# A token-shift layer: who turns the tokens, and on which engine the gate mixture is summed

## The chip, the cores and the metric

The kernel runs on one core of a Trainium2 chip. The metric is the device time of one launch in microseconds. Shown are the median of three runs and, for the profile, one execution taken by the hardware profiler.

The engines are named as the profile names them: PE (TensorE, matrix products), PEld (its weight loads), DVE (VectorE), ACT (ScalarE), POOL (GpSimd) and SP (SyncE, which issues the DMAs). Each works through a queue of its own in order, and waits where an operation needs something that another engine has not delivered yet.

## The reference, cut to what matters

Four layers stand one behind the other, each added to x (8 batches of 512 tokens, 512 features): a cross-attention, a routed feed-forward layer, a masked cross-attention, and the token-shift layer, which the change is about. All is float32.

```python
x_prev = jnp.concatenate([jnp.zeros((B, 1, C)), x[:, :-1, :]], axis=1)
xr = mu_r * x + (1.0 - mu_r) * x_prev          # gate mixture
xk = mu_k * x + (1.0 - mu_k) * x_prev          # key mixture
r = sigmoid(einsum('btc,dc->btd', xr, W_r))    # gates
k_act = square(relu(einsum('btc,dc->btd', xk, W_k)))   # keys
out = r * einsum('btc,dc->btd', k_act, W_v)    # values
...
x = x + tanh(g_ffn[1]) * _L1_ffn_ref(_layernorm(x), W_r, W_k, W_v, mu_r, mu_k)
```

## The kernel before, in words

x stays in SBUF for the whole launch: 32 tiles of 128 tokens by 512 features, four tiles (TB) to a batch. The class ChannelMix is the token-shift layer. It begins inside the second attention: its method in_slot is called from the attention's slots (one slot for each tile; the last four slots and a few behind them are the attention's tail, lines 977 to 994) and prepares batch 0 there. Then mix.run (line 1650) takes the eight batches alone, one after another.

For a batch the layer needs the normalized tokens with features on the partitions. Method normalize (1492) lets ACT write (x - mean) / deviation into a tile xn (line 1500). Method transpose (1504) turns a tile with four PE transposes into one PSUM bank (1514), and ACT copies the bank into yT (1515), a tile of 4 chunks of 128 features by 513 columns whose column 0 is zero, set by POOL (1510): column t+1 holds token t, so that the columns from 0 are the previous tokens and the columns from 1 the tokens themselves. A mixture is made chunk by chunk (mix_chunk, 1517): ACT scales the previous tokens by 1 - mu (1528, "om" is 1 - mu), DVE adds mu times the tokens (1531). xr is the gate mixture, xk the key mixture.

Each of the three 512x512x512 products of a batch (keys, gates, values, in this order) is made by seven products of half the size instead of eight (class SevenProducts). They need sums of quarters of one operand, made beforehand: xks of the key mixture and xrs of the gate mixture (lines 91 to 97 and 107 to 117 make them, so the profile gives them as L91 and L110), wvs of the squared keys. The seven are called p1, p2, p6, p5, p7, p4, p3 in the order in which they run. Each fills one PSUM bank with four matmuls (line 165; the profile counts eight, two passes each) and is taken out of it: p1 and p5 by an ACT copy (177, 192), p2, p6, p7, p4 and p3 by a DVE addition (183, 188, 198, 212, 217). Behind p7, POOL makes two more additions (203, 204); L212 needs the first of them and L217 the second. p6 needs the second sum of its operand's quarters, p5 the first, p7 the third, and p3 or p4 the fourth. Six banks go round.

When a quarter of a product is complete, a function finishes it: the keys get Relu and Square on ACT (1582, 1583), the gates Sigmoid on ACT (1593), the values are multiplied by the gate and r on DVE (1606), added to x on POOL (1609) and, for two quarters together, stored by SP (1618).

The order of the work is written out by hand. A list of seven "turns" holds the steps that are issued behind each of the seven products; method turns (1634) deals a list of steps out evenly, stage (1643) issues them. In run, for batch b:

- key product of b: the four chunks of xr of b (ACT and DVE), then the four sums xrs on DVE; in batches 1 to 4 also the mean and variance (lines 52, 53) of one tile of a later batch behind p2;
- gate product of b: the four sums wvs on DVE, the transposes of the four tiles of b + 1 behind p2, p6, p5 and p7, and the chunks of xk of b + 1;
- value product of b: the four sums xks of b + 1 on DVE, and the normalization of the four tiles of b + 2 on ACT; in batches 0 to 3 the mean and variance of one more tile.

The engines' queues follow this order; SP's queue alone is ordered by the framework. Batch 1 is an exception: its four tiles are normalized behind the attention, at the end of its tail, after the weight sums of the gates (line 1460). The two tiles that hold the normalized tokens of a batch (xn2, two token tiles each) take the places of the attention's v0 and v1.

```python
if b > 0:
    turns = self.turns(chunks(b, 0) + sums(b, 0))
...
for n, step in enumerate(calls(self.transpose, *tiles)):
    turns[n + 1].append(step)
...
work += sums(b + 1, 1)
work += calls(self.normalize, *[(TB * (b + 2) + i,) for i in range(TB)])
```

Of the kernel before, what the change touches and what calls it, by code (L numbers as in the profile page):

```python
# [9 lines left out]
FP = mybir.dt.float32  # L10
I32 = mybir.dt.int32
BF = mybir.dt.bfloat16
AF = mybir.ActivationFunctionType
# [4 lines left out]
P = 128  # L18
B, S, D = 8, 512, 512
LK = 120  # L20
NH, HD = 16, 32
NT = B * S // P
TB = S // P
NC = D // P
# [196 lines left out]
class CrossAttention:  # L221
# [676 lines left out]
    def run(self):  # L898
        for k in range(TB, NT - TB):
            self.steady(k)  # L900
# [96 lines left out]
class RoutedFfn:  # L997
# [101 lines left out]
    def in_slot(self, s, attention, stage):  # L1099

        if stage == "final":
            self.put_aside(s)
            self.route_stats(s)
        if stage == "late":
            self.route_scale(s)
        if stage == 2 and 0 <= s - 1:
            self.route_stats(s - 1)
            self.route_norm(s - 1)
        if stage not in (1, "route"):
            return  # L1110
        pool = attention.p_mm
        if s == -1:
            self.start()
        if stage == "route":
            s -= 1
        if 0 <= s - 4:
            self.route_logits(s - 4, pool.tile([P, D], FP, name="rlps", tag="mm"))
        if 0 <= s - 3:
            self.route_x(s - 3, pool.tile([P, D], FP, name="rxps", tag="mm"))
        b, i = divmod(s - 8, TB)  # L1120
        if i == 0 and 0 <= b < B - 2:
            self.route_back(b, pool.tile([P, D], FP, name="pps", tag="mm"))
# [256 lines left out]
class ChannelMix:  # L1379
# [16 lines left out]
    def start(self):  # L1396
        nc = self.nc
        wr_in, wk_in, wv_in, mu_in = self.ins
        self.pool = pool = self.es.enter_context(
            self.tc.tile_pool(name="cm_w", bufs=1, side="right", reuse_waits="tile")  # L1400
        )
        self.mu = pool.tile([P, 2, NC], FP, name="mu")
        nc.sync.dma_start(out=self.mu, in_=mu_in)
        self.om = pool.tile([P, 2, NC], FP, name="om")
        self.wk = self.load(pool.tile([P, NC, D], FP, name="wk"), wk_in)
        self.wr = self.load(pool.tile([P, NC, D], FP, name="wr"), wr_in)

    def load(self, w, w_in):
        self.nc.sync.dma_start(out=w, in_=w_in.rearrange("(c p) f -> p c f", p=P))
# [26 lines left out]
    def in_slot(self, s, attention, stage):  # L1436

        nc = self.nc
        self.at = attention
        if stage == 2 and s >= 1:  # L1440
            attention.stats(s - 1)
        if stage == "final" and s < NT - 2 * TB:
            attention.stats(s, False)
        if stage == "late" and s < NT - 2 * TB:
            attention.scales(s)
        if s == -1:
            self.start()
        if stage == "head" and s == NT:
            self.sum_value_weights()
            self.k7.next()  # L1450
        if stage == "end" and s == NT + 1:
            for c in range(NC):
                self.mix_chunk(0, 0, c)
            self.k7.next()
        if stage == "end" and s == NT + 2:
            for step in self.sum_steps(0, 0):
                step()
            self.k7.next(2)
            self.sum_gate_weights()
            for t in range(TB, 2 * TB):  # L1460
                self.normalize(t)
        if stage != "route":
            return
        if s == TB + 1:
            nc.vector.tensor_scalar(self.om, self.mu, -1.0, 1.0, ALU.mult, ALU.add)
        i = s - (NT - 9)
        if 0 <= i - 1 < TB:
            self.transpose(i - 1)
        if 0 <= i < TB:
            xn = self.at.norm.tile([P, D], FP, name="xn")  # L1470
            self.normalize(i, xn)
        if s == NT - 4:
            wv = self.at.pool.tile([P, NC, D], FP, name="wv", tag="wq")
            self.wv = self.load(wv, self.ins[2])
            self.weight_sums = self.sum_key_weights()
        if 0 <= s - (NT - 5) < NC:
            self.mix_chunk(0, 1, s - (NT - 5))
        if s in (NT - 4, NT - 3):
            for _ in range(2):
                self.weight_sums.pop(0)()  # L1480
        if s == NT - 2:
            self.key_sums = self.sum_steps(0, 1, nc.gpsimd)
        if s in (NT - 2, NT - 1):
            for _ in range(2):
                self.key_sums.pop(0)()
        if s == NT - 1:
            self.k7 = self.keys(0)
            self.k7.next()
        if s in (NT, NT + 1):
            self.k7.next()  # L1490

    def normalize(self, t, xn=None):
        nc, cm = self.nc, self.cm
        if xn is None:
            i = t % TB
            if i % 2 == 0:
                self.two = self.at.pool.tile([P, 2, D], FP, name="xn2", tag=f"v{i // 2}")
            xn = self.two[:, i % 2, :]
        self.xn[t] = xn
        nc.scalar.activation(  # L1500
            xn, cm.x[:, t, :], AF.Identity, bias=cm.nmr[:, t, :], scale=cm.rstd[:, t, :]
        )

    def transpose(self, t):

        nc = self.nc
        b, i = divmod(t, TB)
        if i == 0:
            self.yT[b] = self.at.work.tile([P, NC, S + 1], FP, name="yT", tag="xnT")
            nc.gpsimd.memset(self.yT[b][:, :, 0:1], 0.0)  # L1510
        xn = self.xn.pop(t)
        ps = self.bank((NC, P))
        for c in range(NC):
            nc.tensor.transpose(ps[:, c, :], xn[:, c * P : (c + 1) * P], self.cm.ident)
        nc.scalar.copy(self.yT[b][:, :, i * P + 1 : (i + 1) * P + 1], ps)

    def mix_chunk(self, b, m, c):

        nc, yT = self.nc, self.yT[b]
        if c == 0:  # L1520
            if m == 1:
                xm = self.at.work.tile([P, NC, S], FP, name="xk", tag="qT")
            else:
                xm = self.at.soft.tile([P, NC * S], FP, name="xr", tag="pr")
                xm = xm.rearrange("p (c s) -> p c s", c=NC)
            self.mix[b, m] = xm
        xm = self.mix[b, m]
        nc.scalar.activation(  # L1528
            xm[:, c, :], yT[:, c, 0:S], AF.Copy, scale=self.om[:, m, c : c + 1]
        )  # L1530
        nc.vector.scalar_tensor_tensor(  # L1531
            xm[:, c, :],
            yT[:, c, 1 : S + 1],
            self.mu[:, m, c : c + 1],
            xm[:, c, :],
            ALU.mult,
            ALU.add,
        )
# [111 lines left out]
    def run(self):  # L1650
        def calls(f, *args):
            return [lambda a=a: f(*a) for a in args]

        def chunks(b, m):
            return calls(self.mix_chunk, *[(b, m, c) for c in range(NC)])

        def sums(b, m):

            steps = []

            def step():
                if not steps:
                    steps.extend(self.sum_steps(b, m))
                steps.pop(0)()

            return [step] * 4

        self.alone = True

        late = NT - 2 * TB  # L1670
        for b in range(B):
            if b > 0:
                turns = self.turns(chunks(b, 0) + sums(b, 0))
                if b <= TB:
                    turns[1].insert(0, lambda t=late + 2 * b - 1: self.at.stats(t))
                self.stage(self.keys(b), turns)
            more = b + 1 < B
            squares = SevenProducts.left_steps(self.kT, *self.kTs, self.nc.vector)
            squares = self.in_order_of_use(squares)
            turns = [[] for _ in range(7)]  # L1680
            for n, step in enumerate(squares):
                turns[n + 2].append(step)
            if more:
                tiles = [(TB * (b + 1) + i,) for i in range(TB)]
                for n, step in enumerate(calls(self.transpose, *tiles)):
                    turns[n + 1].append(step)
                for n, step in enumerate(chunks(b + 1, 1)):
                    turns[5 + n // 2].append(step)
            self.stage(self.gates(b), turns)
            work = []  # L1690
            if more:
                work += sums(b + 1, 1)
            if b + 2 < B:
                work += calls(self.normalize, *[(TB * (b + 2) + i,) for i in range(TB)])
            work = self.turns(work)
            if b < TB:
                work[4].insert(0, lambda t=late + 2 * b: self.at.stats(t))
            self.stage(self.values(b), work)
# [128 lines left out]
```

## Time and profile before

| what | value |
|---|---|
| median of 3 runs | 1346.69 us (1346.25 to 1348.43) |
| the profiled execution, device time | 1344.31 us |
| its span | 1342.5 us |
| PE busy | 1291.0 us, 96% of the span |
| DVE, ACT, POOL busy | 1002.2, 807.1, 704.6 us |
| second attention's tail and what lies around it | about 977 to 1043 us |
| batches 0 to 7 of the token-shift layer alone | about 1039 to 1342 us |

Busy time of an engine is the sum over its instructions; at PE they overlap, and their ends are modelled. In the rows of a timeline or a chain the first number is the start in microseconds from the span's start, the second the length. Where a row ends in square brackets, these hold the idle time of the engine just before the instruction and what ended it. The chain follows the work back from its end: at each step to the instruction that released the waiting one or to the one before it on its engine. "issue" is time in which a queue waits for nothing that the profile shows.

### The profile page before, as it was taken

The numbers are of one execution on the slowest core, as the hardware profiler recorded it, in microseconds if no ns is written. First come the engines' busy times: TensorE is split into PE (matmuls) and PEld (weight loads), VectorE is DVE, ScalarE is ACT, GpSimd is POOL, SyncE is SP. The second block draws the span as 40 slices with busy tenths as digits, with TensorE's granted clock in tenths as the row PEclk, the third lists the DMA queues.
The fourth block names the chain that finished last, engine by engine and source line by source line (L and its number), as shares of the span: only waits on it lengthen the run. The fifth ranks groups of instructions, "written<-read, shape, count | busy, mean of one in ns | idle before, by whom it ended". The sixth has DMA issues, their size and how long they took to land. (4 is left out here: it accounts for less than half of the span.)

```text
span 1342.5 us, 32823 instructions
## 1 busy us (share of the span) xinstructions
PE 1291.0 (96%) x13184; PEld 1024.3 (76%) x13184; DVE 1002.2 (75%) x1448; ACT 807.1 (60%) x2540; POOL 704.6 (52%) x626
## 2 busy tenths in 40 slices
PE   7999999999999988999999999999999999999997
PEld 6886777777766877888888667667666888888886
DVE  5876776777685776777887687777785778787776
ACT  1368888888774445455136778888774655544442
POOL 4856655565542002555797787777664333343332
PEclk9999999999999999999999999999999999999999
DMA  9501766766603256431410077767700000000000
GB/s 313 189 1 66 224 208 204 222 211 208 198 26 111 86 171 199 128 112 63 154 47 18 33 229 214 220 212 222 223 23 1 16 17 32 32 32 32 32 32 32
DMA packets 116237, 160.84 MB, mean 120 GB/s; under 512 B 6973, under 2 KB 71997, under 8 KB 116085
## 3 DMA queue, kind: packets, MB, share of 16 engines
q1 hardware_dynamic: 116085, 158.75, 37.1%
q8 instruction: 104, 1.70, 0.5%
q14 instruction: 48, 0.39, 0.1%
HBM read 93.84 MB, written 64.88 MB: 118 GB/s over the span
## 5 line engine op out<-in xcount | busy, mean ns | idle before, releaser
L721 ACT ACTIVATE pr<-s,nmx 128x120 f32<-128x120 f32 x768 | 273.5, 498 | 43.4 <-DVE nmx L710 25.1
L878 PE MATMUL ops<-wo,aT 128*128 128x512 f32 x512 | 237.0, 604 | 3.6 <-ACT aT L869 2.3
L731 POOL TENSOR_TENSOR pr<-pr,rs 128x960 f32<-128x960 f32 x88 | 160.1, 1820 | 139.9 <-DVE rs L727 138.0
L721 ACT ACTIVATION_READ_ACCUMULATOR pr<-s,nmx 128x1 f32 x768 | 195.3, 254 | 0.0
L878 PEld LDWEIGHTS ops<-wo,aT 128*128 128x128 f32 x512 | 91.9, 189 | 99.8 <-issue 89.2
L710 DVE TENSOR_REDUCE nmx<-s 128x8 f32<-128x960 f32 x96 | 106.6, 1153 | 57.9 <-PE s L666 57.8
L1353 POOL TENSOR_TENSOR r<-r,b 128x1024 f32<-128x1024 f32 x31 | 73.5, 2377 | 145.1 <-ACT r L1352 145.1
L793 DVE STREAM_TRANSPOSE pr<-pr 128x1024 f32<-128x1024 f32 x88 | 109.1, 1240 | 37.0 <-POOL pr L731 37.0
L165 PE MATMUL qps<-xnT,wq 128*128 128x256 f32 x512 | 119.0, 380 | 0.0
L165 PEld LDWEIGHTS qps<-xnT,wq 128*128 128x128 f32 x512 | 96.3, 189 | 23.3 <-issue 10.3
L52 DVE BATCH_NORM_STATS2 bnst<-x 128x6 f32<-128x512 f32 x128 | 87.5, 684 | 0.4
L1609 POOL TENSOR_TENSOR x<-x,cv 128x512 f32<-128x512 f32 x30 | 44.0, 1466 | 79.0 <-DVE cv L1606 79.0
L759 POOL TENSOR_TENSOR pr<-pr,rs 128x960 f32<-128x960 f32 x32 | 58.1, 1823 | 40.6 <-DVE rs L758 30.8
L861 PE MATMUL aps<-prT,v 120*32 120x128 f32 x2048 | 69.2, 276 | 7.6 <-DMA prT<-plane 3.9
L888 DVE SCALAR_TENSOR_TENSOR x<-ops,gates,x 128x512 f32<-128x512 f32 x64 | 47.8, 746 | 34.5 <-PE ops L878 34.1
L666 PE MATMUL s<-kT,qT 32*128 32x120 f32 x2048 | 71.8, 276 | 0.0
L666 PEld LDWEIGHTS s<-kT,qT 32*128 32x128 f32 x2048 | 65.7, 186 | 7.0 <-issue 4.9
L861 PEld LDWEIGHTS aps<-prT,v 120*32 120x32 f32 x2048 | 52.2, 109 | 21.2 <-issue 10.7
L1352 ACT COPY r<-rps 128x1024 f32<-128x1024 f32 x31 | 31.4, 1013 | 59.1 <-PE rps L1340 59.1
L1582 ACT ACTIVATE kT<-kT 128x512 f32<-128x512 f32 x32 | 20.0, 626 | 76.2 <-DVE kT L183 41.8
L1340 PE MATMUL rps<-ident,rT 128*128 128x128 f32 x512 | 61.9, 275 | 2.0 <-DVE rT L1320 1.7
L769 ACT ACTIVATE pr<-s,nmx 128x120 f32<-128x120 f32 x128 | 44.2, 371 | 29.0 <-DVE nmx L766 29.0
(239 smaller groups left out, 3134.4 us busy)
## 6 DMA issues: line engine op xcount, KB each, us to landing
plane<-pr SPq DMA_DIRECT2D x88, 512.0 KB, 3.5
prT<-plane SPq DMA_DIRECT2D x176, 240.0 KB, 4.1
w<-in_w_dram SPq DMA_DIRECT2D x32, 512.0 KB, 5.0
x<-in_x_dram SPq DMA_DIRECT2D x8, 1024.0 KB, 16.6
aside<-x SPq DMA_DIRECT2D x32, 256.0 KB, 3.1
x<-aside SPq DMA_DIRECT2D x8, 1024.0 KB, 9.7
out_dram<-x SPq DMA_DIRECT2D x14, 512.0 KB, 2.8
wk<-in_wk_dram SPq DMA_DIRECT2D x3, 1024.0 KB, 8.8
```

The costliest lines, as they stand in the source:

```text
L52: cm.nc.vector.bn_stats(st, cm.x[:, t, :])
L165: self.nc.tensor.matmul(ps[:, m, :], rows[:, k, m * n : (m + 1) * n], columns[:, k, :], start=(k == 0), stop=(k == 1),)
L666: nc.tensor.matmul(s[j // 2][:, j % 2, hc * LK : (hc + 1) * LK], self.qT[b][r : r + 32, hc, toks], self.kT[r : r + 32, hc, keys], start=no ...
L710: nc.vector.tensor_reduce(nmx[u], sv[u], AX.X, ALU.max, negate=True)
L721: nc.scalar.activation(dst, src, AF.Exp, bias=nmx[u][:, j, hc, :], accum_out=sm[:, u, j, hc : hc + 1],)
L731: nc.gpsimd.tensor_tensor(half[u], half[u], by, ALU.mult)
L759: nc.gpsimd.tensor_tensor(pr[:, js, :, :], pr[:, js, :, :], rs[:, js, :, :].to_broadcast([P, 2, NC, LK]), ALU.mult,)
L793: nc.vector.transpose(pr, pr)
L861: nc.tensor.matmul(out, self.v[b // 2][:LK, b % 2, h * HD : (h + 1) * HD], p, start=True, stop=True,)
L878: nc.tensor.matmul(ops, self.aT[t][:, c, :], self.wo[:, c, :], start=(c == 0), stop=(c == NC - 1),)
L1340: nc.tensor.transpose(ps[:, k // 4, (k % 4) * P : (k % 4 + 1) * P], self.rT[:, 16 * tq + 8 * h + k, :], self.cm.ident,)
L1353: nc.gpsimd.tensor_tensor(r, r, b2, ALU.add)
```

## The change

Features change their order inside the layer: on partition 32q + e, chunk j now stands feature 128q + 32j + e. So the weights of keys and gates (load_rows) and mu are loaded in that order, by 16 DMAs instead of three, and the tokens of batch 0, which PE still turns, are written in that order by their normalization.

From batch 1 on, a pair of normalized tiles is stored to DRAM and loaded again in four DMAs, by blocks of 32 tokens by 128 features, so that each block of 32 partitions holds 32 x 32 pieces that belong there (move_rows). DVE then turns all 32 x 32 blocks of a tile in one instruction straight into yT. PE's transposes, their PSUM banks and ACT's copies of them go.

The four sums xrs are made by POOL instead of DVE. The scaling of the gate mixture (ACT) is issued in the value product of the batch before, the addition (DVE) stays in the key product. Batch 1 is normalized in two slots of the attention's tail, two tiles in each.

```diff
+        for m in range(2):
+            by_row = mu_in[:, m, :].rearrange("(j e) q -> q e j", j=NC)
+            for q in range(4):
+                nc.sync.dma_start(out=self.mu[32 * q : 32 * q + 32, m, :], in_=by_row[q])
...
+    def load_rows(self, w, w_in):
+        rows = w_in.rearrange("(q j e) f -> q e j f", q=4, j=NC)
+        for q in range(4):
+            self.nc.sync.dma_start(out=w[32 * q : 32 * q + 32], in_=rows[q])
+        return w
...
-            for t in range(TB, 2 * TB):
-                self.normalize(t)
...
         if s in (NT - 4, NT - 3):
-            for _ in range(2):
+            for n in range(2):
                 self.weight_sums.pop(0)()
+                self.normalize(TB + 2 * (s - NT + 4) + n)
...
+        if not moved:
+            to = xn.rearrange("p (j q e) -> p q j e", q=4, j=NC)
+            x = x.rearrange("p (q j e) -> p q j e", q=4, j=NC)
...
+    def move_rows(self, t):
+        nc = self.nc
+        plane = self.at.dram.tile([2 * P, D], FP, name="rows")
+        nc.sync.dma_start(out=plane.rearrange("(i p) d -> p i d", p=P), in_=self.two)
+        two = self.at.pool.tile([P, 2, D], FP, name="xn2", tag=f"v{t % TB // 2}")
+        quarters = plane.rearrange("(i e) (q d) -> q e i d", e=32, q=4)
+        for q in range(4):
+            nc.sync.dma_start(
+                out=two[32 * q : 32 * q + 32].rearrange("p i (q d) -> p (i q) d", q=4),
+                in_=quarters[q],
+            )
...
+        if b > 0:
+            to = self.yT[b][:, :, i * P + 1 : (i + 1) * P + 1]
+            nc.vector.transpose(
+                to.rearrange("p j (q t) -> p q j t", q=4),
+                xn.rearrange("p (q j e) -> p q j e", q=4, j=NC),
+            )
+            return
...
-                turns = self.turns(chunks(b, 0) + sums(b, 0))
+                turns = self.turns(chunks(b, 0, self.mix_add) + sums(b, 0, self.nc.gpsimd))
...
             if more:
                 work += sums(b + 1, 1)
+                work += chunks(b + 1, 0, self.mix_scale)
```

mix_scale and mix_add are the two halves of mix_chunk, which calls both where they stay together.

More of the change, by code (lines that the diff above doesn't have):

```diff
@@ L1402, in start @@
         self.mu = pool.tile([P, 2, NC], FP, name="mu")
-        nc.sync.dma_start(out=self.mu, in_=mu_in)
+        for m in range(2):
+            by_row = mu_in[:, m, :].rearrange("(j e) q -> q e j", j=NC)
+            for q in range(4):
+                nc.sync.dma_start(out=self.mu[32 * q : 32 * q + 32, m, :], in_=by_row[q])
         self.om = pool.tile([P, 2, NC], FP, name="om")
-        self.wk = self.load(pool.tile([P, NC, D], FP, name="wk"), wk_in)
-        self.wr = self.load(pool.tile([P, NC, D], FP, name="wr"), wr_in)
+        self.wk = self.load_rows(pool.tile([P, NC, D], FP, name="wk"), wk_in)
+        self.wr = self.load_rows(pool.tile([P, NC, D], FP, name="wr"), wr_in)
+    def load_rows(self, w, w_in):
[3 more added lines that the diff above has]
+        return w
     def load(self, w, w_in):
@@ L1493, in normalize @@
         nc, cm = self.nc, self.cm
-        if xn is None:
-            i = t % TB
+        moved = xn is None
+        i = t % TB
+        if moved:
             if i % 2 == 0:
@@ L1499, in normalize @@
         self.xn[t] = xn
+        to, x = xn, cm.x[:, t, :]
+        if not moved:
+            to = xn.rearrange("p (j q e) -> p q j e", q=4, j=NC)
+            x = x.rearrange("p (q j e) -> p q j e", q=4, j=NC)
         nc.scalar.activation(
-            xn, cm.x[:, t, :], AF.Identity, bias=cm.nmr[:, t, :], scale=cm.rstd[:, t, :]
+            to, x, AF.Identity, bias=cm.nmr[:, t, :], scale=cm.rstd[:, t, :]
         )
+        if moved and i % 2:
+            self.move_rows(t - 1)
+    def move_rows(self, t):
[9 more added lines that the diff above has]
+            )
+        for n in range(2):
+            self.xn[t + n] = two[:, n, :]
     def transpose(self, t):
@@ L1517, in mix_chunk, with mix_scale @@
     def mix_chunk(self, b, m, c):
-        nc, yT = self.nc, self.yT[b]
+        self.mix_scale(b, m, c)
+        self.mix_add(b, m, c)
+    def mix_scale(self, b, m, c):
         if c == 0:
@@ L1526, in mix_chunk, with mix_add @@
             self.mix[b, m] = xm
+        self.nc.scalar.activation(
+            self.mix[b, m][:, c, :], self.yT[b][:, c, 0:S], AF.Copy,
+            scale=self.om[:, m, c : c + 1],
+        )
+    def mix_add(self, b, m, c):
         xm = self.mix[b, m]
[L1528 to L1531, printed above, removed]
+        self.nc.vector.scalar_tensor_tensor(
             xm[:, c, :],
-            yT[:, c, 1 : S + 1],
+            self.yT[b][:, c, 1 : S + 1],
             self.mu[:, m, c : c + 1],
@@ L1652, in calls, with chunks, sums @@
             return [lambda a=a: f(*a) for a in args]
-        def chunks(b, m):
-            return calls(self.mix_chunk, *[(b, m, c) for c in range(NC)])
-        def sums(b, m):
+        def chunks(b, m, f=self.mix_chunk):
+            return calls(f, *[(b, m, c) for c in range(NC)])
+        def sums(b, m, engine=None):
             steps = []
@@ L1662, in step @@
                 if not steps:
-                    steps.extend(self.sum_steps(b, m))
+                    steps.extend(self.sum_steps(b, m, engine))
                 steps.pop(0)()
```

## The prediction

> **What bounds the kernel now.** I read the page's busy times, then the same engines by stage, then the chain that ended last within one batch, then each engine's timeline. The change works in the last 300 us, where the token-shift layer runs alone, one batch of 38.7 us after another. Two batches by stage:
>
> ```profile
> core 0: us, PE busy (x) PEld busy (x) DVE busy (x) ACT busy (x) POOL busy (x), PEclk, DMA share, GB/s
> 1132.41:1171.15 38.74, 38.57 (x186) 33.46 (x185) 31.47 (x44) 20.12 (x35) 14.10 (x11) 1.00 0.07 28
> 1171.15:1209.91 38.76, 38.58 (x186) 33.46 (x185) 31.47 (x43) 20.12 (x35) 16.07 (x15) 1.00 0.08 28
> ```
>
> PE looks full, at the full clock. Counted from the starts of its instructions its work is less: 21 products at 1.73 are 36.25, four groups of transposes (L1514) at 0.44 are 1.76, together 38.0; the other 0.7 is waiting, behind the second and third transposes. And the chain of the same batch, back to where it began, holds no PE at all. An excerpt (start, length, what):
>
> ```profile
> 1152.08 0.61 DVE kT L183
> ...
> 1152.71 0.64 ACT kT L1582
> ...
> 1153.91 0.71 ACT xr L1528
> ...
> 1154.65 0.75 DVE xr L1531
> ...
> 1156.00 0.67 DVE xr L1531
> ...
> 1156.69 0.69 DVE xrs L91
> 1157.39 0.61 DVE kT L198
> ...
> 1158.13 1.60 POOL kT L203
> ...
> 1163.43 0.48 ACT r L177
> ...
> 1163.93 0.70 DVE r L183
> ...
> 1164.72 0.69 DVE r L188
> ...
> 1166.74 0.67 DVE r L198
> ...
> 1167.54 1.59 POOL r L203
> ...
> 1169.15 0.70 DVE r L212
> ```
>
> The reader is to see a loop: DVE hands to ACT, ACT to DVE, DVE to POOL, POOL to ACT (the square of the keys, 1159.75 to 1163.43), ACT to DVE, and 38.73 later the same pieces again. Two limits lie almost on each other: PE's work of 38.0 and this loop of 38.73. Taking the transposes off PE lowers the first to 36.25 and moves nothing by itself; the new length of the loop decides.
>
> **The loop, piece by piece.** A DVE operation on 512 columns starts 0.60 after the one before (0.66 for L1531 and L1606), or 0.72 after one that it depends on.
>
> (a) The gate mixture's scaling goes to the value product. Now the third L1531 of xr waits for L183, then ACT's L1582 and L1583, then L1528: 1152.08 to 1154.65, 2.57. Afterwards L183 alone stands ahead of it, 0.60: minus 1.97. But in the key products of batches 1 to 4 a tile's statistics (L52, L53: 0.72 and 0.18, at 1191.35) stand there too. Today they lie in that wait and are free; then they are on the loop, and the gain is 1.07. The four L1528 cost nothing in their new place: ACT idles 3.4 before the next keys' L177.
>
> (b) The sums on POOL. Now from the last L1531 (1156.00) DVE does one sum and L198, and POOL's L203 ends at 1159.73: 3.73. Then POOL makes the first sum itself, ahead of L203 in its queue: 0.78 + 1.24 + 1.29 (POOL rows at 1181.63 and 1182.86) = 3.31, minus 0.42. The other three DVE sums filled waits for POOL (1.17) and ACT (1.23), so their going gains nothing. Queued behind POOL's new sums are the memset of yT and the next L203 of r, which has 6.5 of idle time before it.
>
> POOL's second sum stands behind L203 and L204, and PE's third gate product needs it: 0.78 + 4 x 1.24 = 5.7 after the last L1531 starts. By PE's own pace that is some 2 to 3 us late, so PE idles there about as long as the transposes had cost it. The loop just misses this: r's L188 needs that product 8.7 after the same start, and it is done at 7.7; L198 needs the product two later at 11.8, and it is done at 11.2.
>
> (c) The turning on DVE. Three of the four new transposes stand between r's L183 and L198, the fourth in the wait for POOL. The nearest row is the attention's:
>
> ```profile
> L793 DVE STREAM_TRANSPOSE pr<-pr x88: 1229/1240/1249, 122.1 to 963.3; 128x1024 f32<-128x1024 f32 x88
> ```
>
> 1024 columns start to start take 1.17 (957.81 to 958.98), so 512 take about 0.64 if time goes by columns, and its narrow spread says that POOL does not disturb it. Bounds: 0.60, as any operation here on 512 columns, and 1.24, the whole row, if the new write in pieces of 32 columns with a long stride halves the pace. I take 0.64: the same operation, the same blocks. L183 to L198 is 2.81 now, then 4 x 0.60 + 3 x 0.64 = 4.32: plus 1.51. Its waits for DMA (two with four queues each) add small steps of 0.02 on DVE (the DVEq rows): plus 0.1.
>
> [...]
>
> (d) The value product. Twelve steps instead of eight are dealt out over its seven products, so the sums come two by two and L188 of cv follows the fourth xks sum instead of hiding in it. That sum waits until POOL's L1609 ends, since a DVE operation with two SBUF inputs and a POOL operation exclude each other (L91 at 1160.35 takes 1.15 while L204 runs, 0.68 otherwise): plus 0.60 + 0.12 = 0.71.
>
> Sum for a batch: -1.97 - 0.42 + 1.51 + 0.10 + 0.71 = -0.1 without statistics, +0.8 with them. PE's 36.25 stays below both.
>
> **The ends.** Start: four normalizations (L1500, 2.83) leave ACT's queue at 1042.87, where r's L177 and behind it L183 (1046.30) waited; L183 then comes after DVE's last weight sum, about 1043.65: minus 2.65. Then four batches at +0.8 and two at -0.1: +3.0. The last batch has no transposes and PE carries it as today, from one product earlier: level. Together +0.4 for the layer, within 1.5 either way.
>
> The normalizations move to two slots of the attention's tail, between L1528 and L869 on ACT:
>
> ```profile
> 994.58 0.76 ACT L1528 ACTIVATE xk<-yT,om 128x512 f32<-128x512 f32 x1
> 995.20 0.62 ACT L869 COPY aT<-aps 128x512 f32<-128x512 f32 x1
> 995.87 0.65 PE L840 MATMUL tps<-ident,pr 128*120 128x128 f32 x4 [0.20 <-ACT aT L869]
> ```
>
> PE already waits for that copy to free a bank. Two normalizations at 0.73 push it by 1.45, the last transposes, the scores, the maxima and the exponentials after it by some 1.35: twice, plus 2.7. PE has no idle time from 1005 to 1042 in which to win it back.
>
> Costed at nothing, with the cover: eight small loads of mu and eight of the weights on SP (about 0.4 each, at 684 to 702) have 59 us until SP's next work at 760.91; bounds are nothing and, without that cover, 16 x 0.4 = 6.4. The moved tokens: on SP two stores (512 KB, 3.5 to landing), four loads, the two output stores, four loads. The second loads stand behind the output stores and so behind the last L1609, some 10 us after the key product's start; six issues at about 0.6 (the loads at 648 to 653 take 0.35 to 0.6) and 4.1 to land (the prT row) end by 18, and the third transpose wants them at 24. Each us beyond that margin of 6 would be a us on the loop. The permuted write of batch 0's tokens on ACT: the same columns, nothing.
>
> **The sum.** The profiled execution took 1344.31 for a span of 1342.5. 1344.3 + 0.4 + 2.7 = 1347.4. The median of the three runs shown is 1346.69; carried over to it, the same +3.1 gives **1349.8**. A measurement here can tell about 0.2%, 2.7 us, from no change.
>
> **Rivals.**
> *PE was the limit (faster).* The loop has slack that the chain hides, for instance because (b) and (d) cost less, and a batch falls to PE's 36.25. Each of seven batches then gains 1.76 + 0.7 = 2.5, 17 in all; less the tail's 2.7: 1346.7 - 14.6 = 1332. For it: PE is 99% busy. Against it: the chain has no PE in 38.7 us. It decides in full where (c) and (d) together add nothing; each 0.1 a batch on the way there is 0.7 us.
> *The transpose costs 1.24.* Three on the loop, 1.8 a batch, seven batches 12.6: 1349.8 + 12.6 = 1362. For it: the strided write that no row shows. Against: L793.
> *The tail absorbs the normalizations.* ACT idles 2 us before L769 in each slot; if PE's order lets the copy come late, 1347. Against: the 0.20 above.
>
> **How the numbers follow.** Forecast 0.50 (1346 to 1354: slower 0.27, within 0.20, faster 0.03), PE the limit 0.22 (faster), dear transpose 0.18 (slower), tail absorbed 0.10 (within 0.08, faster 0.02). Faster 0.27, within 0.28, slower 0.45. The range reaches about to the middles of both outer rivals, 1333 to 1361, and leaves out half of each, 0.20.
>
> **What will show it.** A batch of 38.6 or 39.5 us, the longer ones with statistics; PE with 2 to 3 us of idle time a batch before the third gate product, ended by POOL's xrs; the new transpose at 0.7 us; L183 of r some 2.6 earlier at the layer's start against the tail; two tail slots 1.35 longer. A batch below 38 would prove me wrong on the loop, a transpose over 1 us on (c), DVE waiting for a DMA on the loads.

## The result, and the profile after

| | before | after |
|---|---|---|
| median | 1346.85 us, 4 runs (1346.25 to 1348.43) | 1355.20 us, 4 runs (1354.03 to 1358.73) |
| ratio | | 1.0063, 95% interval 1.0042 to 1.0084 |
| profiled execution, span | 1344.31, 1342.5 us | 1354.03, 1352.2 us |
| mean granted clock of it | 0.999 | 0.994 |

The change makes the kernel slower by 8.4 us, 0.6%. The forecast was 1349.8, with a chance of 0.50 on 1346 to 1354. The side is right. The time lies 1.2 above that band and inside the wide range of 1333 to 1361, and 5.4 us are missing.

Two batches of the kernel after, by stage, from one L212 of r to the next (columns as in the rows of before: busy time of each engine, granted clock, share and rate of DMA):

```profile
core 0: us, PE busy (x) PEld busy (x) DVE busy (x) ACT busy (x) POOL busy (x), PEclk, DMA share, GB/s
1095.97:1136.89 40.92, 38.22 (x170) 33.03 (x169) 31.45 (x44) 18.26 (x31) 20.79 (x20) 0.96 0.25 77
1136.89:1176.13 39.24, 36.90 (x172) 32.16 (x171) 31.31 (x43) 18.26 (x31) 18.67 (x16) 1.00 0.27 81
```

The second row is the batch of the forecast, 39.2 against 39.5. The first is 1.7 longer, about 0.35 of it through POOL (see the smaller misses below), and the column to look at for the rest is the clock: 0.96. PE's busy time is higher in it too, though its work is the same. The chain of the first row, from the key product on, no longer closes over DVE, ACT and POOL alone (start, length, what):

```profile
1118.42 0.60 DVE kT L183
1119.02 0.62 DVE bnst L52
...
1119.92 0.65 POOL ve L61
...
1120.64 1.05 POOL rstd L62
...
1123.48 1.26 POOL kT L203
1124.74 1.23 POOL kT L204
1125.97 1.25 POOL xrs L91
1127.21 0.04 issue
1127.26 9.94 PE cps L165 x37
```

The statistics (L52) stand on it as forecast in (a), their scales on POOL (L61, L62) follow, which no step had counted, POOL makes its second xrs behind L203 and L204 as forecast in (b), and then PE, which the forecast had kept off the path, carries ten microseconds. PE's third gate product in batches 1 to 4, from PE's timeline (in brackets the idle time before it and what ended it):

```profile
1086.34 7.13 PE L165 MATMUL cps<-wrs,xrs 128*128 128x256 f32 x24 [2.31 <-POOL xrs L91]
1127.26 7.13 PE L165 MATMUL cps<-wrs,xrs 128*128 128x256 f32 x24 [2.70 <-POOL xrs L91]
1167.81 5.45 PE L165 MATMUL cps<-wrs,xrs 128*128 128x256 f32 x24 [2.34 <-POOL xrs L91]
1207.40 6.90 PE L165 MATMUL cps<-wrs,xrs 128*128 128x256 f32 x24 [3.06 <-POOL xrs L91]
```

The idle time is what (b) forecast, 2 to 3 us. What it did not forecast is the length, in the second column: the same three products take 5.45 in one batch and 6.9 to 7.1 in three others. Windows around the first, third and fourth of these gaps show why:

```profile
1084.08:1087.49 3.41, 1.15 (x5) 1.05 (x6) 1.16 (x2) 3.31 (x7) 3.41 (x4) 1.00 0.00 0
1087.49:1090.91 3.42, 3.42 (x9) 2.71 (x9) 2.89 (x5) 1.13 (x3) 1.31 (x3) 0.50 0.00 0
1090.91:1094.32 3.41, 3.41 (x17) 2.99 (x16) 2.21 (x5) 0.59 (x1) 0.00 (x0) 1.00 0.01 2
...
1166.00:1169.42 3.42, 1.61 (x7) 1.44 (x8) 0.71 (x2) 3.36 (x6) 3.42 (x4) 1.00 0.00 0
1169.42:1172.83 3.41, 3.41 (x17) 3.01 (x16) 3.34 (x6) 1.26 (x3) 0.85 (x2) 1.00 0.00 0
1203.55:1206.96 3.41, 0.79 (x4) 0.36 (x2) 1.37 (x2) 1.97 (x4) 3.41 (x4) 1.00 0.00 0
1206.96:1210.38 3.42, 2.98 (x7) 2.44 (x8) 1.29 (x2) 2.63 (x5) 2.89 (x4) 0.50 0.00 0
```

After the first and the last of these gaps PE has half the clock for 3.41 us: 9 matmuls instead of 17 in the same time (7 in the last one, which begins with 0.43 of idle time). Such a stretch is called a dip below. Behind the slow products r's L198 waits for PE on DVE, as in before it did in batch 0 alone (1.38 at 1050.48):

```profile
1093.51 0.69 DVE L198 TENSOR_TENSOR r<-r,cps 128x512 f32<-128x512 f32 x1 [1.20 <-PE cps L165]
```

The parts of the profiled execution, measured (after less before) beside the forecast:

| stretch | forecast | measured |
|---|---|---|
| up to the first of the two tail slots | 0 | +2.4 |
| from there to the first L212 of r: two tail slots +2.7, layer's start -2.65 | +0.05 | +0.1 (+2.7, -2.8, and +0.2 from L183 to L212) |
| four batches with statistics (38.75 became 40.53, 40.92, 39.24, 40.67) | +3.2 | +6.4 |
| two without (38.7 became 38.46, 38.80) | -0.2 | -0.2 |
| last batch to the end (57.12 became 58.14) | 0 | +1.0 |

The first row is not the change's: at 525 us, long before any changed instruction, this execution was late by 2.35 already; the twelve profiled executions of this study spread over 7.7 us there, and that of the kernel before is the earliest. Without this row the change costs 7.3 in the profile against a forecast of 3.1, so 4.2 of the missing 5.4 us show there; the rest is less than this spread.

### The profile page after: what moved, and what is told of

Same layout as the page of the kernel before. It is cut to its first block, busy times and chain, and to the rows that moved or that the text cites. A ratio compares the mean times of both kernels' runs of the same rounds, so it can differ in the third digit from the quotient of the medians.

```text
span 1352.2 us, 32815 instructions
## 1 busy us (share of the span) xinstructions
PE 1282.6 (95%) x13072; PEld 1016.6 (75%) x13072; DVE 1001.0 (74%) x1448; ACT 794.4 (59%) x2512; POOL 736.9 (54%) x654
## 5 line engine op out<-in xcount | busy, mean ns | idle before, releaser
L721 ACT ACTIVATE pr<-s,nmx 128x120 f32<-128x120 f32 x768 | 273.5, 498 | 43.2 <-DVE nmx L710 23.6
L710 DVE TENSOR_REDUCE nmx<-s 128x8 f32<-128x960 f32 x96 | 106.6, 1152 | 58.2 <-PE s L666 58.1
L793 DVE STREAM_TRANSPOSE pr<-pr 128x1024 f32<-128x1024 f32 x88 | 109.1, 1240 | 36.9 <-POOL pr L731 36.9
L52 DVE BATCH_NORM_STATS2 bnst<-x 128x6 f32<-128x512 f32 x128 | 87.5, 684 | 0.4
L165 PE MATMUL cps<-wrs,xrs 128*128 128x256 f32 x192 | 48.4, 414 | 15.8 <-POOL xrs L91 15.7
```

The lines of the kernel that those rows point to most:

```text
L52: cm.nc.vector.bn_stats(st, cm.x[:, t, :])
L165: self.nc.tensor.matmul(ps[:, m, :], rows[:, k, m * n : (m + 1) * n], columns[:, k, :], start=(k == 0), stop=(k == 1),)
L710: nc.vector.tensor_reduce(nmx[u], sv[u], AX.X, ALU.max, negate=True)
L721: nc.scalar.activation(dst, src, AF.Exp, bias=nmx[u][:, j, hc, :], accum_out=sm[:, u, j, hc : hc + 1],)
L793: nc.vector.transpose(pr, pr)
```

## The experiments

The theory after the comparison: the loop came out as forecast, and the missing microseconds are PE's clock, which falls after the idle time that POOL's late second sum leaves. The rival: the loop itself is 40.5 long, through the transposes or through POOL's sums, and the clock only follows. All ratios are to the kernel before, run beside each experiment on the same chip (median 1350.07 in the first four, 1348.12 in the next four, 1348.88 in the last two). Batches are given as periods of L212 of r, batch 0 first.

**The changed kernel once more**, unaltered.

> The changed kernel once more, unaltered, on the chip of the next three, so that they are compared on one chip. Both theories: about 1355 (1354 to 1359). Clock theory: the granted clock of the profiled execution is below 0.997, and every batch over 40 us has it below 0.9 in the stretch after the third gate product's idle time; a batch without the dip is 38.5 to 39.7. Loop theory: batches of 40.5 and more also where the clock stays at 1.00.

1358.03 us, 6 runs, 1.0065 (1.0043 to 1.0087). Periods 40.52, 40.90, 40.54, 40.90, 38.46, 40.10, 37.58. In every one over 40 the three products behind the gap take 7.13 again, in the others 5.45: five dips in all. In the execution above there were three, and the seven periods added up to 276.2 against 279.0 here. The execution's clock is 0.988; five dips at 0.50 take 0.006 off it, so the rest lies outside these periods.

**Useless work into the gap.** The bank of the third gate product is filled once before with another product.

```diff
     def p6(self):
-        ps = self.multiply("S2", "T2")
+        ps = self.filler() if self.fill else None
+        ps = self.multiply("S2", "T2", ps)
...
+    def filler(self):
+        return self.multiply("A11", "B11")
```

"fill" is set for the gates of batches 1 to 7, and multiply takes the bank that it is given.

> One more product (first quarter times first quarter, 1.73 us at PE) into the same bank, ahead of the third gate product of batches 1 to 7, which then overwrites it: useless work that lies in PE's idle time of 1.4 to 3.1 us and leaves 0 to 1.4 of it. Clock theory: PE is never idle long enough to be throttled; three batches give back 1.27, 1.27 and 1.02, so 1355.2 - 3.6 = 1351.6 (1350.5 to 1352.5), granted clock 0.998 or more, batches 38.5 and 39.2 to 39.7, none over 40. Loop theory (the transposes and POOL's sums make the loop longer by themselves): no change, 1355, or slower by the filler where the idle time is shorter than 1.73 (0.3 in the last batch).

1352.59 us, 12 runs, 1.0023 (1.0009 to 1.0037): 5.4 us below the unaltered kernel beside it, by PE doing 12 us more. The mean clock of these runs is 0.994 to 0.998, that of the six unaltered ones 0.988 to 0.993. Expected was 0.998 or more; the profiled execution has 0.996, with no dip in the layer. From its windows and from PE's timeline:

```profile
1058.32:1097.54 39.22, 38.61 (x179) 33.67 (x178) 31.33 (x43) 18.26 (x31) 18.68 (x16) 1.00 0.26 81
1097.54:1137.12 39.58, 38.26 (x178) 33.36 (x177) 31.32 (x43) 18.25 (x30) 20.73 (x20) 1.00 0.26 80
```
```profile
1089.24 5.45 PE L170 MATMUL cps<-wrs,xrs 128*128 128x256 f32 x24 [0.61 <-POOL xrs L91]
1128.81 5.45 PE L170 MATMUL cps<-wrs,xrs 128*128 128x256 f32 x24 [1.32 <-POOL xrs L91]
```

No dip in the layer in this execution, the three products at 5.45 in every batch, periods 39.22, 39.58, 39.25, 39.59, 38.46, 38.82, 37.60. The seven add up to 272.5, against 276.2 with three dips and 279.0 with five: 1.2 and 1.3 us a dip. This settles the clock against the rival: nothing was altered on DVE, ACT or POOL, whose transposes and sums are still there, and the batches over 40 are gone.

**The sums on DVE again**, all else as changed.

```diff
-   turns = self.turns(chunks(b, 0, self.mix_add) + sums(b, 0, self.nc.gpsimd))
+   turns = self.turns(chunks(b, 0, self.mix_add) + sums(b, 0))
```

> The four sums of the gate mixture are made by DVE again, all else as changed. Clock theory: the third gate product is not late any more; PE's idle time of a batch (38.7 less 36.25, 2.4) is split over several products, most often ahead of the second ones, into pieces under 2.0, and the clock stays. Gains: 3.6 of clock and 0.8 of POOL's scales in two batches; loss: term (b), 0.42 in each of seven batches, 2.9. 1355.2 - 4.4 + 2.9 = 1353.7 (1352.5 to 1355). Loop theory with POOL's sums as the cause (they keep DVE and POOL off each other's way): batches of 38.6 everywhere, 1355.2 - 8 = 1347. Loop theory with the transposes as the cause: 1358.

1351.09 us, 12 runs, 1.0015 (1.0000 to 1.0029): 6.9 us below the unaltered kernel, more than the clock theory gave. Two of its batches and the waits of its PE:

```profile
1140.22:1179.87 39.65, 37.53 (x170) 31.51 (x169) 34.19 (x47) 17.94 (x31) 14.09 (x12) 1.00 0.26 80
1219.55:1258.41 38.86, 37.04 (x170) 31.68 (x169) 32.65 (x44) 17.94 (x31) 14.08 (x12) 1.00 0.26 81
```
```profile
1152.60 1.99 PE L165 MATMUL cps<-xk,wk 128*128 128x256 f32 x8 [1.52 <-DVE cv L188]
1168.04 5.42 PE L165 MATMUL cps<-wrs,xrs 128*128 128x256 f32 x24 [0.45 <-DVE xrs L91]
```

As expected, PE's idle time is split, into pieces of 1.52 at most, and no dip follows: the clock is 1.00 in all seven periods. The loop is 0.45 longer than with the filler in batch 1 (39.67 against 39.22), 0.40 in batch 3 and, without statistics, in batch 5: there term (b), -0.42, was right. In batches 2, 4 and 6, which POOL's sums delay in other ways (see the smaller misses), it is 0.04 to 0.11. What I had left out is the end: the last period and the rest behind it are 36.60 + 18.13 = 54.7, against 37.60 + 20.56 = 58.2 with POOL's sums. In the last batch nothing is turned, so L183 to L198 is short, and POOL's late sums meet it.

**Batch 1's normalization behind the copy of aT**, in the same two tail slots.

```diff
         if s in (NT - 4, NT - 3):
...
-                self.normalize(TB + 2 * (s - NT + 4) + n)
+        if stage == "end" and s in (NT - 4, NT - 3):
+            for n in range(2):
+                self.normalize(TB + 2 * (s - NT + 4) + n)
```

> Batch 1 is normalized in the same two slots of the attention's tail, but issued behind the copy of aT instead of ahead of it, where ACT waits some 2 us for the next transposes. My step on the tail: the two slots fall from 9.46 to about 8.1 each, minus 2.7 in all, 1352.5, and the layer's start stays as changed. Rival (the slots are longer for another reason, such as the new DMAs beside them): the slots stay at 9.4, 1355. A second rival: the copies that follow the normalizations are late by as much, and half comes back, 1353.8.

1354.61 us, 11 runs, 1.0039 (1.0025 to 1.0053), 3.4 below the unaltered kernel beside it; the 1352.5 expected was worked out from the first result, 1355.2. The last transposes of a slot, in the kernel after and here:

```profile
991.55 0.65 PE L840 MATMUL tps<-ident,pr 128*120 128x128 f32 x4 [1.52 <-ACT aT L869]
```
```profile
998.71 0.65 PE L840 MATMUL tps<-ident,pr 128*120 128x128 f32 x4 [0.19 <-ACT aT L869]
```

The two slots are some 9.5 each in the kernel after, 8.1 each here, and the layer's start did not move back. The step on the tail was right to a tenth. The profiled execution has five dips (five periods at 0.96, the products behind their gaps at 7.13), as the unaltered one beside it.

**The scaling back into the key product**, on top of the sums on DVE, so that the turning is nearly all that is left of the change.

```diff
-   turns = self.turns(chunks(b, 0, self.mix_add) + sums(b, 0))
+   turns = self.turns(chunks(b, 0) + sums(b, 0))
...
-                work += chunks(b + 1, 0, self.mix_scale)
```

> Compared with the kernel whose gate sums are on DVE again (1351.1 where before was 1350.1; batches of 39.67 with statistics, 38.86 without): the scaling of the gate mixture goes back into the key product as well, so that of the change the turning on DVE and the place of batch 1's normalization are left. My terms (a) and (d): +1.97 without statistics or +1.07 with them, -0.71: batches of 40.0 (the first four) and 40.1, together +5.2 over seven batches, 1.0055 of before. Rival (DVE's transposes alone make the loop 39 to 40 and the scaling is hidden in DVE's own work): batches stay at 39.7 and 38.9. PE is idle for 3.8 us a batch here, so the clock may fall too; then single batches are 1.3 longer, and the clock row says which.

1354.92 us, 4 runs, 1.0058 (1.0036 to 1.0081). A batch with statistics and one without:

```profile
1135.83:1175.97 40.14, 37.96 (x170) 31.35 (x169) 33.63 (x47) 18.06 (x30) 14.10 (x12) 1.00 0.25 79
1216.09:1256.22 40.13, 37.95 (x170) 31.35 (x169) 32.05 (x43) 18.06 (x30) 14.08 (x12) 1.00 0.25 79
```

40.13 in all, so the early scaling is worth 1.27 without statistics and 0.46 with them; (a) and (d) together had said 1.26 and 0.36. The turning on DVE, with the rest of a batch's work as before, makes a batch 1.4 longer (38.74 before); term (c) had said 1.6.

**PE turns again**, on top of the sums on DVE: the early scaling without the transposes on DVE.

```diff
-        if moved and i % 2:
-            self.move_rows(t - 1)
...
-        if b > 0:
-            to = self.yT[b][:, :, i * P + 1 : (i + 1) * P + 1]
...
-            return
```

> Compared with the same kernel (gate sums on DVE, 39.67 and 38.86): the tokens of all batches are turned by PE again and copied by ACT, nothing is moved by DMA; the early scaling is left, with the normalization's place. Theory of two limits: the loop loses term (c), 1.61, and falls to 38.1 and 37.3, PE has 38.0 of work again and is the limit: batches of 38.0 to 38.1, the same with and without statistics, clock 1.00, PE idle under 0.3 a batch; together some 5 to 7 less than the kernel with DVE's sums, 0.997 of before. Rival (the transposes on DVE are hidden in its waits, as the idle time of DVE suggests): 39.7 and 38.9 stay, 1.0015.

1345.64 us, 10 runs, 0.9982 (0.9967 to 0.9997).

```profile
1132.33:1170.57 38.24, 38.24 (x186) 33.50 (x185) 32.02 (x43) 20.14 (x35) 14.06 (x12) 1.00 0.07 28
1208.85:1246.87 38.02, 38.02 (x186) 33.49 (x185) 30.53 (x39) 20.23 (x34) 14.09 (x12) 1.00 0.08 28
```

Without statistics (the second row) busy time equals the period, and it is PE's own 38.0: the early scaling takes the loop below PE's work, and there PE really is the limit. With statistics 0.2 more are left. Of the parts tried alone, the turning and this one, only this one pays by itself.

**Four corrections together**: sums on DVE, normalization behind aT, the key product's statistics behind the fifth product, and the four scalings dealt out last.

```diff
-                    turns[1].insert(0, lambda t=late + 2 * b - 1: self.at.stats(t))
+                    turns[4].append(lambda t=late + 2 * b - 1: self.at.stats(t))
...
-                work += chunks(b + 1, 0, self.mix_scale)
...
             work = self.turns(work)
+            if more:
+                for n, step in enumerate(chunks(b + 1, 0, self.mix_scale)):
+                    work[5 + n // 2].append(step)
```

> Gate sums on DVE; the normalization behind the copy of aT; the statistics of the key product behind the fifth product, into DVE's wait for POOL; the four early scalings dealt behind the sixth and seventh value product, so that the sums xks stand as before the change. Theory: what these parts cost adds up: tail -2.7, statistics -0.8 in four batches, dealing (term d) -0.71 in seven: -2.7 - 3.2 - 5.0 = -10.9 against the kernel with DVE's sums alone, batches of 37.4 to 38.1, 0.994 of before. Rival (each was hidden already, the loop closes over something else): only the tail's 2.7, batches 38.9, 1.000 of before.

1337.87 us, 4 runs, 0.9925 (0.9908 to 0.9942). Six periods of 38.06 to 38.10, with statistics or without: these cost nothing in their new place (0.8 before), and the dealing, term (d), was worth 38.86 - 38.07 = 0.79 against 0.71 forecast.

**And the sums of the squared keys later**, by two, two, one and one product, so that fewer operations stand between r's L183 and L198.

```diff
-            for n, step in enumerate(squares):
-                turns[n + 2].append(step)
+            for n, step in zip((4, 5, 5, 6), squares):
+                turns[n].append(step)
```

> As the kernel with all four corrections, and the first three sums wvs of the squared keys issued two or three products later, behind L198, so that between r's L183 and L198 DVE has three transposes and one sum fewer than two. Theory of the loop: 1.2 less on it, 36.9 at most, and PE's own 36.25 becomes the limit in some batches: batches of 36.3 to 36.9, PE idle under 0.7, 7 to 8 less than the kernel with four corrections, 0.988 of before, so that the relief of PE is paid out at last. Rival (the loop closes over ACT or over the value product, which now waits for its sums): batches of 37.5 to 38.1, no gain over the kernel with four corrections.

1334.85 us, 4 runs, 0.9912 (0.9889 to 0.9935). A batch of the four corrections, and one of this kernel:

```profile
1206.07:1244.14 38.07, 37.33 (x170) 31.50 (x169) 31.95 (x44) 17.95 (x31) 14.08 (x12) 1.00 0.28 83
```
```profile
1201.29:1238.45 37.16, 36.73 (x169) 31.67 (x168) 31.88 (x43) 18.06 (x30) 14.10 (x12) 1.00 0.28 85
```

37.16 instead of the expected 36.9 at most: L183 to L198 fell by 1.20, from 4.22 to 3.02, but the batch by 0.91, and the chain of a batch still runs over DVE, ACT and POOL without PE. The trace shows where 0.3 came back: one of the moved sums now stands ahead of DVE's first addition for xk, which starts 2.28 after r's L212 instead of 2.00. The last batch lost 1.1 (35.63 + 20.07 against 36.49 + 18.11).

**One matmul of filler** in the changed kernel, in the place of the whole product.

```diff
     def filler(self):
-        return self.multiply("A11", "B11")
+        ps = self.psum()
+        rows, columns = self.a["A11"], self.b["B11"]
+        self.nc.tensor.matmul(
+            ps[:, 0, :], rows[:, 0, 0:P], columns[:, 0, :], start=True, stop=True
+        )
+        return ps
```

> The changed kernel with one matmul (0.43 us) of useless work ahead of the third gate product, instead of a whole product. The idle times before that product, 2.31, 2.70, 2.34, 2.69 or 3.06, 1.56, 2.27 and 1.05 to 1.43 in the runs of the changed kernel, become some 1.9, 2.3, 1.9, 2.3 to 2.6, 1.1, 1.8 and 1.0 at most. Theory of the window: the clock is halved for 3.41 us when PE was idle for over 2.0 to 2.2 us of one piece of a fixed grid of 3.41 us (the runs of the changed kernel: 2.22 to 2.68 in a piece before each of 12 dips, 2.00 at most in the others). So only batches 2 and 4 can still dip: 0 to 2 dips instead of 3 to 5, each 1.3, and the kernel takes 1.0032 +- 0.001 of before. Rival 1 (any gap at that place dips, the length matters little): 5 dips, 1.006. Rival 2 (the filler's whole length was needed for another reason, such as the weights it keeps loaded): 1.006 as well, without a rule by length.

1355.53 us, 4 runs, 1.0048 (1.0031 to 1.0066). The interval holds the rivals' 1.006 too, so the time decides nothing, and there are three dips where 0 to 2 were expected. What the gaps show is in PE's timeline:

```profile
1088.89 5.45 PE L175 MATMUL cps<-wrs,xrs 128*128 128x256 f32 x24 [1.89 <-POOL xrs L91]
1128.48 7.13 PE L175 MATMUL cps<-wrs,xrs 128*128 128x256 f32 x24 [2.63 <-POOL xrs L91]
1169.06 7.13 PE L175 MATMUL cps<-wrs,xrs 128*128 128x256 f32 x24 [1.93 <-POOL xrs L91]
1209.97 7.13 PE L175 MATMUL cps<-wrs,xrs 128*128 128x256 f32 x24 [2.26 <-POOL xrs L91]
```

The third contradicts my boundary of 2.0 to 2.2: 1.93 was enough here. No dip followed the gaps of 1.89 and 1.84, which is against rival 1. Rival 2 is not excluded by this run.

**The last batch's sums where the change has them**, otherwise as the kernel with later sums.

```diff
-            for n, step in zip((4, 5, 5, 6), squares):
+            places = (4, 5, 5, 6) if more else (2, 3, 4, 5)
+            for n, step in zip(places, squares):
```

> As the kernel with all corrections and the later sums of the squared keys, but in the last batch, which has nothing behind it to be turned, these sums stay where the change has them. Theory: from L212 of the last gates to the end it took 20.07 with the later sums and 18.11 without, while its period was 35.63 against 36.49: 1.1 less in all, batches of 37.16 as before, 0.990 of before. Rival: the end hangs on PE, no difference.

1335.36 us, 4 runs, 0.9896 (0.9877 to 0.9914). In the profile the last batch is 36.75 + 18.12 = 54.87 against 55.70: 0.8 of the 1.1 expected; the medians can't tell the two kernels apart. Both beat the kernel before by 1%, some 13 us.

## Why the prediction was right, and where it failed

**Right by its steps.** The turning: 0.70 us for one, 0.63 from start to start, forecast 0.64, and L183 to L198 takes 4.22, forecast 4.32. From the groups by line (count; shortest, median and longest in ns):

```profile
L1545 DVE STREAM_TRANSPOSE yT<-xn x28: 698/702/705, 1049.2 to 1292.8; 128x512 f32<-128x512 f32 x28
```

0.70 for every one of the 28, which write in pieces with a long stride, disposes of the rival that it costs 1.24. No DVE operation waited for the moved rows, so the loads were rightly costed at nothing. (a) with (d) came out at 1.27 and (d) at 0.79, both without statistics, (b) at 0.40 to 0.45 in batches 1, 3 and 5; the statistics cost 0.8. Without dips the batches are 39.2 to 39.6 and 38.5 to 38.8, forecast 39.5 and 38.6. The tail is +2.7, the start -2.8. Without dips in the layer (the filler) the kernel stands at 1.0023 of before, 3.1 us (1.2 to 5.0), as the forecast's sum. Part of that is luck: by the periods of the profile, six batches cost 2.5 where 3.0 was forecast, and the last one 1.0 where nothing was.

**Where it failed.** The step is in (b): "PE idles there about as long as the transposes had cost it. The loop just misses this". The length of the idle time was right, 2.3 to 3.1 in the batches with statistics, and so was the margin of 0.6 with which L198 misses PE's delay: without a dip it doesn't wait (batches 3, 5 and 6), and with one it waits 1.20 behind products that are 1.68 longer (7.13 less 5.45), which leaves a margin of 0.5 (behind the 6.90 in batch 4 it waits 0.35). But the step let PE run at full pace behind its idle time, as it does in before, where PE waits some 0.3 at a time (1122.71 to 1123.41 is 0.70 from the start of L1514 to the next product, 1120.54 to 1120.98 is 0.44) and the granted clock is 1.00 from 1045 to 1338 us. It doesn't here: what a dip takes beyond the margin comes out at L198 and goes round the loop, 1.1 to 1.3 each. Three dips are 3.7 us in the profiled execution, five are 6.5 in the other one: this is most of what was missing. A margin of 0.6 should have been priced as gone, as I did with other covers.

**Smaller misses.** (b) forgot that in batches 2 and 4 POOL's scales (L61 to L67, 2.3 us) stand ahead of its first xrs; these batches are about 0.35 longer than their neighbours. Batch 6 is longer by as much for another reason: PE is so late that in the value product ahead of it L198 waits for PE, 0.46 in the kernel after, without any dip. And "PE carries it as today" in the last batch failed: with no transposes in it, POOL's sums are on its path, +1.0 against before, and 3.4 against the same sums on DVE. So POOL's sums as a whole lose 1.9 us against sums on DVE by the filler's periods (-1.5 over six batches, +3.4 at the end), before any dip.

**The rivals.** "PE was the limit" was wrong of this change and right of its early scaling: alone it ends at PE's 38.0. Once the other parts stood where they are covered, with the sums back on DVE, the turning paid as well: 37.16, below PE's own 38.0 with the transposes on it. "The tail absorbs the normalizations" is wrong ahead of the copy of aT and right behind it.

## What to carry to other kernels

Taking work off an engine that is nearly full gained nothing here until the loop beside it got shorter, and each piece that is moved should go where its new engine waits: with the sums back on DVE and the other pieces in other places of the queues, +0.6% became -1.0%. Idle time on TensorE was not free here, though nobody waited for it at the moment: price what its next products cost at half pace (here 7.13 us instead of 5.45 behind gaps of 1.93 to 3.06), and where a gap can't be closed, useless work in it can be cheaper than the gap, as one product was here (5.4 us less in all); one matmul was not enough (three dips were left). When a batch is longer than its neighbour at the same work, look at the granted clock around each gap before looking for new work.

## What the runs showed of the hardware

**A fixed grid for the clock.** In the three profiled executions of the changed loop with these gaps unfilled (the changed kernel twice, and with its normalization moved) 13 dips fall into the layer's work, by the 6.90 to 7.13 us of the three products behind the gap (5.45 in the other batches). In the kernel after each lasts 3.41 us at 0.50, and between them lie whole multiples of 3.413: 1087.49 to 1128.46 above is 12 of them, 1128.46 to 1206.96 is 23, while the gaps in front of them end 40.92 and 80.14 apart. So in this execution the dips stand on a grid of time that doesn't follow the program. In the pieces of the grid just ahead of the three dips PE idled 2.26, 2.22 and 2.62 us; the most where none followed is 1.99 (1282.05 to 1285.47: 3.42 less PE's 1.43). This fits the third gate product at 1167.81: its gap of 2.34 is as long as the first one, but lies across two pieces, with 1.81 in the larger.

By the whole gap, 2.26 to 3.06 us stand in front of the 13 dips and 1.93, 2.26 and 2.63 in front of the three with the small filler. Gaps of 2.34 and 2.27 in the kernel after, and all gaps of 1.89 or less in the layer, were followed by none. With the small filler a gap of 1.93 was enough, and in the kernel after 1.99 of one piece was not, so idle time as the profile counts it is not the whole rule; what else counts was not tried.

These figures are those of the layer's seven periods alone. Outside them the clock falls too: in the kernel after it is 0.50 from 1346.91 us to the end of the span, where PE has no work left, and the 0.988 of the changed kernel's second execution is more than its five dips (0.006) and such an end (0.002) take.

**The loop may lock to the grid.** Twelve pieces are 40.96 us (40.97 between the first two dips of the kernel after). A batch with statistics and a dip takes 40.5 to 40.9, so the next gap falls on nearly the same place in the grid and dips again (four in a row in the second profile, behind gaps that end at 1087.40, 1128.29, 1168.84 and 1209.74), while a batch of 39.2 moves the gap by 1.7 us in the grid and gets away. No run moved the grid against the loop, so this is argued and not shown.
